# A quantizer's levels redistributed over three engines, with a transposed router product and a reordered hand-over between two phases

## The chip, the cores and the metric

The kernel runs on one core of a Trainium2 chip. The metric is the device time of one execution in microseconds (us). The engines are named as the profile names them: PE is TensorE (matrix products), DVE is VectorE, ACT is ScalarE, POOL is GpSimd, and SP is SyncE, whose queue only issues transfers here. Each engine executes its own instructions in the order in which the program wrote them; engines wait for each other through semaphores.

## The reference

All values are fp32. A weight matrix of 2048 x 2048 is quantized to a codebook of 32 values, and the result is multiplied on to two further matrices before it meets the 4096 tokens:

```python
lora_delta = lora_B @ lora_A * 0.5
cb = codebook / max(|codebook|)
normalized = (weight + lora_delta) grouped by 128 / exp(scale_log)
idx = searchsorted((cb[:-1] + cb[1:]) / 2, normalized)      # 31 thresholds
w = (cb[idx] - normalized) + normalized
w_eff = w * scale + lora_delta
y = x @ w_eff.T
...
result = y @ W_base.T + b_base
ax, probs = y @ A_w.T, softmax(y @ router_w.T)               # 16 and 8 columns
mixed = sum over experts of probs[e] * (ax @ cores[e])
out = x + result + mixed @ B_w.T * 2
```

## The kernel before

The kernel folds the matrices together first. **Phase one** forms the combined weight W_base times w_eff (plus the identity, which brings the "x +"), and the 24 router columns (16 of A_w, 8 of router_w) times w_eff. **Phase two** multiplies the tokens by the combined weight, in a two-level Strassen-like scheme of 49 block products for each of 4 token groups (line 902), which read their weights as pieces `s` from a scratch tensor `s_dram` in DRAM.

Phase one walks over 16 strips of w_eff, i = 0 to 15, each 128 x 2048. A strip lies in two tiles: `w`, the normalized weights, and `a`, the quantized result. The quantizer raises `a` from the lowest codebook value through the 31 sorted thresholds: a level r adds the r-th rise wherever w lies above the r-th threshold. For most levels this is a pair (`raise_to`, lines 527 to 535): ACT makes a mask from `w` by a Relu against the threshold, in bf16, and DVE copies the next value into `a` under the mask. Two mask buffers exist, so ACT can be at most about one mask ahead of DVE. One such pair is called a **step** here; the first copy of a strip is step 0.

The lowest levels of strip i+1 are done during strip i by other means. Before the change these are levels 0, 1 and 2: ACT does level 0 in three operations on each half of the strip (`level_0`, lines 505 to 514: Relu, Sign, then scale and bias into `a`), POOL does levels 1 and 2 on each half with a compare-and-multiply into `lv` and an add into `a` (`more_levels`, lines 516 to 522). So strips 1 to 15 have 28 steps, r = 3 to 30. Strip 0 starts at r = 2.

The order of all other work is written out by hand: `behind(n, f, ...)` (line 719) puts a call into the program after step n of strip i, and so into the queue of every engine that the call uses. During strip i, the following run beside the copies:

- For strip i+1: its load (`load_w`), the low-rank part on PE (`delta`), its scaling on ACT (`scaled`, line 496) and normalizing on POOL (`normalize`, lines 498 to 501), then the lowest levels.
- For strip i-1: after the last copy POOL finishes a strip by `straight_through` (lines 544 to 554, three operations on each half). PE then multiplies its `a` with four column blocks of W_base, first the pair (2, 0), then the pair (3, 1), each in four chunks c = 0 to 3 (`products`, line 703, with `multiply` at line 594 and `low_rank` with its products at line 589). The last chunk of (3, 1) runs at the start of strip i+1. Between the pairs comes `multiply_router` (lines 609 to 616).
- Each of these five results lies in one of only three rotating PSUM buffers. ACT empties them: `keep` (line 618) copies one column block out and SP stores it to the scratch tensor `wc_dram`; `keep_router` (line 623) copies the router's columns to `rac`. In strip i the blocks 3 and 1 of strip i-2 are kept at steps 5 and 6, the blocks 2 and 0 of strip i-1 at steps 17 and 19, the router at 22.
- `load_route` and `route` (lines 627 to 645): four transfers of 512 KB of x, and 8 products of the router columns with them, for a whole strip at once.
- From strip 5 on POOL forms Strassen sums of finished columns (`outer_w`, `inner_pair`), which are fetched (`fetch`, line 303) and stored to `s_dram` (`put`, line 340).

**The passage** stands between the phases. The last strips' columns must go through `wc_dram`, be fetched (`late_columns`, line 677; `last_fetch` for the blocks 1 and 3, line 1127), summed on DVE and put to `s_dram` through POOL's queue, while SP also issues the loads of x (xA, xB, xC) and of `s` for the first products of line 902. Three `s` buffers exist; product n uses piece s_n, and `load_s(n + 3)` stands behind product n in the program. Lines 1127 to 1141 give the order: s_0 to s_2, then `last_fetch(1)`, `last_fetch(3)`, then the load of xB.

Of the kernel before, what the change touches and what calls it, by code (L numbers as in the profile page):

```python
# [20 lines left out]
P = 128  # L21
BIG = 3.0e38
LORA_SCALE = 32.0 / 64.0
MIX_SCALE = 32.0 / 16.0


def quantizer_tables(nc, work, const, psum, cb, index, beside):
# [107 lines left out]
    base = const.tile([P, 5], F32, name="base")  # L135
    v.tensor_tensor(base[:, 0:1], step[:, 0:1], cb[:, 0:1], ALU.subtract)
    next(beside, None)
    v.tensor_copy(base[:, 2:3], step[:, 0:1])
    next(beside, None)
    v.tensor_tensor(base[:, 1:2], step[:, 1:2], base[:, 2:3], ALU.subtract)  # L140
    next(beside, None)
    v.tensor_copy(base[:, 3:4], step[:, 1:2])
    next(beside, None)
    v.tensor_tensor(base[:, 3:4], step[:, 2:3], base[:, 3:4], ALU.subtract)
    next(beside, None)
    v.tensor_scalar(base[:, 2:5:2], neg_t[:, 1:3], -1.0, None, ALU.mult)
    next(beside, None)
    return neg_t, step, base
# [34 lines left out]
def adaln_ffn_kernel(  # L183
# [72 lines left out]
    nc.gpsimd.memset(rac, 0.0)  # L256
    cb = const.tile([P, K], F32, name="cb")
    ident = const.tile([P, P], F32, name="ident")
    ones = const.tile([P, 1], F32, name="ones")

# [7 lines left out]
    def constants():  # L268
        make_identity(nc, ident)
        nc.gpsimd.memset(cores_sb, 0.0)  # L270

        nc.gpsimd.tensor_copy(ones, ident[:, Q : Q + 1])
        for j in range(1, 4):
            nc.gpsimd.tensor_tensor(ones, ones, ident[:, RP * j + Q : RP * j + Q + 1], ALU.add)
        for j in range(4):
            nc.sync.dma_start(cores_sb[:, j, 0:Q], cores)
            for rows, what in ((slice(RP * j, RP * j + Q), bwT), (slice(RP * j + Q, RP * j + Q + 1), bias)):
                nc.sync.dma_start(
                    bw_sb[rows].rearrange("q (f n) p -> q f n p", n=2),
                    what.rearrange("q (f j n p) -> q j f n p", j=4, n=2, p=P)[:, j],  # L280
                )
# [21 lines left out]
    def fetch(g, b):  # L303
        for j in range(4):
            ih, col = j // 2, j % 2
            nc.sync.dma_start(
                cols[g, b]["up"][:, ih::2, col],
                wc_dram[g][b][:, j].rearrange("p (h a) c -> p h a c", a=2),
            )
# [52 lines left out]
    with ExitStack() as sa:  # L362
# [4 lines left out]
        xsp = sa.enter_context(tc.tile_pool(name="xsp", bufs=4))  # L367
# [61 lines left out]
        with tc.tile_pool(name="tables", bufs=1) as tables:  # L429
# [20 lines left out]
            neg_t, step, base = quantizer_tables(nc, tables, const, psum_t, cb, index, first_scales)  # L450
# [23 lines left out]
        ra_sb = cl.tile([P, NM, NRA], F32, name="ra_sb")  # L474
        nc.sync.dma_start(ra_sb, raT)
# [29 lines left out]
        def level_0(i, f, part):  # L505
            q, a = half(i, f, "w"), half(i, f, "a")
            if part == 0:
                strips[i]["sg"] = mpool0.tile([P, NM // 2, P], BF16, tag="sg", name=f"sg_{i}_{f}")
                nc.scalar.activation(strips[i]["sg"], q, AF.Relu, bias=neg_t[:, 0:1])  # L509
# [3 lines left out]
            if part == 2:  # L513
                nc.scalar.activation(a, sg, AF.Identity, bias=cb[:, 0:1], scale=base[:, 0:1])  # L514

        def more_levels(i, f):
            a = half(i, f, "a")
            lv = mpool0.tile([P, NM // 2, P], F32, tag="lv", name=f"lv_{i}_{f}")
            v = nc.gpsimd
            for c in (1, 3):  # L520
                v.tensor_scalar(lv, half(i, f, "w"), base[:, c + 1 : c + 2], base[:, c : c + 1], ALU.is_gt, ALU.mult)  # L521
                v.tensor_tensor(a, a, lv, ALU.add)  # L522
# [14 lines left out]
        def quantize(i, at):  # L537

            for r in range(3 if i else 2, T):
                raise_to(i, r, new_mask(i, r), 0, 1)  # L540
                for do in at.get(r - 3, []):
                    do()

# [14 lines left out]
        lora_r = cl.tile([R, NRA], F32, name="lora_r")  # L558
# [19 lines left out]
        def lora_router():  # L578
            ps = psum_m.tile([P, OQ], F32, tag="m", name="lc_r")
            for m in range(NM):  # L580
                nc.tensor.matmul(
                    ps[:R, :NRA], lora_B_sb[:, m, :], ra_sb[:, m, :], start=(m == 0), stop=(m == NM - 1)
                )
            nc.scalar.mul(lora_r, ps[:R, :NRA], LORA_SCALE)
# [24 lines left out]
        def multiply_router(i):  # L609
            ps = psum_m.tile([P, OQ], F32, tag="m", name=f"m_{i}_r")  # L610
            for m in range(NM):
                nc.tensor.matmul(
                    ps[:, :NRA], strips[i]["a"][:, m, :], ra_sb[:, m, :], start=(m == 0), stop=False
                )
            nc.tensor.matmul(ps[:, :NRA], strips[i]["la"][:R], lora_r, start=False, stop=True)
            strips[i]["r"] = ps

# [5 lines left out]
        def keep_router(i):  # L623
            nc.scalar.copy(rac[:, strip[i], 0:NRA], strips[i]["r"][:, :NRA])


        def load_route(i):
            strips[i]["x"] = []
            for n in range(4):
                x = xsp.tile([P, 2 * HT], F32, tag="xs", name=f"xs_{i}_{n}")  # L630
                nc.sync.dma_start(x, xT[ts(strip[i], P), ts(n, 2 * HT)])
                strips[i]["x"].append(x)

        def route(i):
            for n in range(8):
                j = n % 4
                nc.tensor.matmul(
                    acc[n // 4][RP * j : RP * j + RP],
                    rac[:, strip[i], :],
                    strips[i]["x"][n // 2][:, ts(n % 2, HT)],  # L640
# [36 lines left out]
        def late_columns():  # L677

            t = big0.tile([P, NM, OQ], F32, tag="wb", name="late").rearrange("p m o -> p (m o)")
            for n, b in enumerate((0, 2)):  # L680
                f = t[:, 3584 * n : 3584 * n + 3584]
                columns(NK - 1, b, f[:, 0:2048], f[:, 2048:3584])
                fetch(NK - 1, b)
            for b in (0, 2):
# [12 lines left out]
                last_put(b, (5, 6), (2, 7), (3,), (4,))  # L697

# [17 lines left out]
        for i in range(NS):  # L716
# [5 lines left out]
            if i > 1:  # L722

                products(i - 2, (3, 1), NC - 1)
                route(i - 2)
                behind(5, keep, i - 2, 3)
                behind(6, keep, i - 2, 1)
            if i + 1 < NS:
# [5 lines left out]
                for f, (a, b, c) in enumerate(((10, 12, 14), (16, 18, 20))):  # L734
                    behind(a, level_0, i + 1, f, 0)
                    behind(b, level_0, i + 1, f, 1)
                    behind(c, level_0, i + 1, f, 2)
                    behind(c, more_levels, i + 1, f)
                behind(11, scaled, i + 1, 1)
                behind(11, normalize, i + 1, 1)  # L740
            if i > 0:


                behind(9, load_route, i - 1)
                for c in range(2):
                    behind(2 + 3 * c, products, i - 1, (2, 0), c)
                if i + 1 < NS:
                    behind(7, delta, i + 1, 1)
                for c in range(2, NC):
                    behind(2 + 3 * c, products, i - 1, (2, 0), c)  # L750
                behind(13, multiply_router, i - 1)
                behind(17, keep, i - 1, 2)
                behind(19, keep, i - 1, 0)
                for c in range(NC - 1):
                    behind((17, 20, 22)[c], products, i - 1, (3, 1), c)
                behind(22, keep_router, i - 1)
                if i + 2 < NS:
                    behind(20, load_la, i + 2)
            else:
# [3 lines left out]
                behind(24, lora_columns, 1)  # L763
                behind(26, lora_router)
            for n, (g, b) in enumerate(made.get(i, [])):
                step_of = (4, 9, 11, 12, 15, 26, 27) if len(made[i]) == 1 else (
# [31 lines left out]
        route(last - 1)  # L798
        keep(last - 1, 3)
        keep(last - 1, 1)  # L800
        load_route(last)
# [4 lines left out]
        for bs in ((2, 0), (3, 1)):  # L806
            for c in range(NC):
                products(last, bs, c)
            if bs[0] == 2:
                multiply_router(last)  # L810
            for b in bs:
                keep(last, b)
            if bs[0] == 2:
                keep_router(last)
                late_columns()
        route(last)
# [286 lines left out]
    at(early, 1, lambda g: load_x("xC", g, 1, 1))  # L1103
# [23 lines left out]
    def last_fetch(b, t):  # L1127
        buf = home[t].tile([P, 4096], F32, tag=t, name=f"last_{b}")
        columns(NK - 1, b, buf[:, 0:2048], buf[:, 2048:3584])
        fetch(NK - 1, b)  # L1130
# [8 lines left out]
    last_fetch(1, "C12")  # L1139
    last_fetch(3, "U2")  # L1140
    load_x("xB", 0, 0, 1)
# [18 lines left out]
    for n in range(total + 1):  # L1160
# [12 lines left out]
        if n + 3 < total and n < total:  # L1173
            load_s(n + 3)
        if 1 <= n <= total:
# [52 lines left out]
```

## Time and profile before

Three runs took 2699.41, 2703.0 and 2703.13 us; the median is 2703.0. The profiled execution took 2701.32 us, with a span of 2699.5 and a mean granted TensorE clock of 0.971.

| engine | busy us | share of the span | instructions |
|---|---|---|---|
| PE matmul | 2562.5 | 95% | 10544 |
| PE weight load | 1761.5 | 65% | 10544 |
| DVE | 1574.9 | 58% | 995 |
| ACT | 1117.8 | 41% | 740 |
| POOL | 1300.1 | 48% | 751 |

| operation, shape | engine | count | mean ns |
|---|---|---|---|
| masked copy, 128x2048 (line 533) | DVE | 449 | 2479 |
| mask, 128x2048 (line 532) | ACT | 449 | 1998 |
| Relu, Sign, scale and bias, 128x1024 (509, 512, 514) | ACT | 30 each | 1133, 1043, 1231 |
| compare and multiply, 128x1024 (521) | POOL | 60 | 3782 |
| add, 128x1024 (522) | POOL | 60 | 2375 |
| column block out of PSUM, 128x512 (620) | ACT | 64 | 568 |

A duration in such a table is the time from an operation's start to its end. Operations of one engine can overlap a little, so where they run back to back the distance from start to start counts, and it is shorter: a mask takes 1998 ns, but the next operation starts 1.90 us after it. The page's shares are averages over two phases with different limits: DVE is busy nine tenths and more of each slice until about 1190 us, and two to four tenths afterwards. Ends of matmuls are modelled, so PE's 95% does not say that PE is the limit.

### The profile page before, as it was taken

To read this page: it belongs to the slowest core of one execution; us is meant where nothing else is said; L and a number is where in the kernel's file an instruction comes from. 1 tells how busy PE (TensorE), PEld (TensorE's weight loads), DVE (VectorE), ACT (ScalarE), POOL (GpSimd) and SP (SyncE) were. 2 spreads that over 40 slices of the span, in tenths; PEclk is the share of its full clock that TensorE was granted. 3 is DMA by queue.
4 is the path that set the end of the run, shared out by engine and by line. 5 is a ranking of instruction groups with operands and counts; after the bars stand their busy time and mean duration, and the time that the engine had idled before them with its cause. 6 is when DMAs were issued, how large, how long until landed. Compare 5 with 4: busy or idle time off the path is not lost.

```text
span 2699.5 us, 26233 instructions
## 1 busy us (share of the span) xinstructions
PE 2562.5 (95%) x10544; PEld 1761.5 (65%) x10544; DVE 1574.9 (58%) x995; ACT 1117.8 (41%) x740; POOL 1300.1 (48%) x751
## 2 busy tenths in 40 slices
PE   4699999999999999999799999999999999999999
PEld 2244444444444444445688888888888888888887
DVE  9999999999999999973423213233123322224321
ACT  6888988999998888840000000000000000000000
POOL 5666668889888888744304232033310313302324
PEclk9799999999999999999899999999999999999999
DMA  7345457766776767699744666545675455854554
GB/s 283 138 167 178 178 174 246 233 229 225 244 242 232 244 219 237 209 314 324 300 174 143 231 245 217 208 142 209 213 264 186 171 206 181 292 194 171 186 198 163
DMA packets 222809, 581.06 MB, mean 215 GB/s; under 512 B 18328, under 2 KB 120608, under 8 KB 177760
## 3 DMA queue, kind: packets, MB, share of 16 engines
q1 hardware_dynamic: 216448, 559.01, 60.2%
q0 software_dynamic: 4640, 13.90, 1.4%
q10 hardware_dynamic: 1600, 6.49, 0.6%
q8 instruction: 83, 1.36, 0.2%
q14 instruction: 38, 0.31, 0.0%
HBM read 477.62 MB, written 101.71 MB: 215 GB/s over the span
## 4 chain that ended last, share of the span: by engine, by line
PE 59%; DVE 22%; ACT 8%; DMA 5%; issue 3%; SPq 2%; POOL 1%; DVEq 0%; POOLq 0%; ACTq 0%
PE z L902 49%; DVE a L533 21%; PE m L601 8%; ACT above L532 6%; PE z L932 1%; DMA wbp<-in_wbT 1%; DMA s<-s_dram 1%; DMA xA<-in_xT 1%; ACT out L620 1%; DMA s_dram<-late_z 1%; ACT a L514 1%; SPq L347 1%; SPq L348 0%; DMA s_dram<-z 0%; ACT sg L509 0%
## 5 line engine op out<-in xcount | busy, mean ns | idle before, releaser
L533 DVE COPY_PREDICATED a<-above,step 128x2048 f32<-128x2048 uint16 (+1 forms) x453 | 1116.5, 2468 | 51.1 <-ACT above L532 5.7
L532 ACT ACTIVATE above<-w,neg_t 128x2048 bf16<-128x2048 f32 (+1 forms) x453 | 899.4, 1991 | 141.7 <-DVE a L533 128.8
L902 PE MATMUL z<-t,s 128*128 128x256 f32 x3584 | 793.5, 381 | 7.1 <-DMA s<-s_dram 7.1
L902 PEld LDWEIGHTS z<-t,s 128*128 128x128 f32 x3584 | 679.1, 190 | 110.9 <-issue 20.0
L601 PE MATMUL m<-wbp,a 128*128 128x512 f32 x1024 | 506.7, 641 | 43.0 <-POOL a L554 35.7
L601 PE MATMUL m<-wb,a 128*128 128x512 f32 x1024 | 467.0, 599 | 26.6 <-ACT out L620 26.6
L601 PEld LDWEIGHTS m<-wbp,a 128*128 128x128 f32 x1024 | 205.7, 206 | 294.4 <-issue 243.9
L601 PEld LDWEIGHTS m<-wb,a 128*128 128x128 f32 x1024 | 194.7, 192 | 276.6 <-issue 238.7
L982 ACT COPY m<-z 128x1024 f32<-128x1024 f32 x28 | 28.4, 1013 | 766.0 <-PE z L902 766.0
L902 PE MATMUL z<-xA,s 128*128 128x256 f32 x1152 | 256.2, 381 | 12.4 <-DMA s<-s_dram 12.4
L993 POOL TENSOR_TENSOR c<-u,m 128x1024 f32<-128x1024 f32 x16 | 50.1, 3129 | 444.1 <-DVE u L990 422.8
L902 PEld LDWEIGHTS z<-xA,s 128*128 128x128 f32 x1152 | 219.8, 191 | 43.7 <-issue 13.6
L521 POOL TENSOR_SCALAR lv<-w,base 128x1024 f32<-128x1024 f32 x60 | 226.9, 3782 | 3.7
L993 POOL TENSOR_TENSOR M<-u,m 128x1024 f32<-128x1024 f32 x8 | 25.7, 3208 | 354.1 <-DVE u L990 296.4
L902 PE MATMUL z<-xB,s 128*128 128x256 f32 x768 | 169.7, 379 | 0.0
L902 PE MATMUL z<-xC,s 128*128 128x256 f32 x768 | 169.7, 379 | 0.0
L984 DVE TENSOR_TENSOR u<-z,m 128x1024 f32<-128x1024 f32 x28 | 34.3, 1223 | 219.0 <-issue 175.5
L902 PEld LDWEIGHTS z<-xB,s 128*128 128x128 f32 x768 | 145.9, 190 | 19.8
L902 PEld LDWEIGHTS z<-xC,s 128*128 128x128 f32 x768 | 145.9, 190 | 19.8
L988 ACT COPY m<-z 128x1024 f32<-128x1024 f32 x28 | 28.3, 1011 | 308.5 <-PE z L902 308.5
L522 POOL TENSOR_TENSOR a<-a,lv 128x1024 f32<-128x1024 f32 x60 | 142.5, 2375 | 18.4 <-ACT a L514 13.8
L552 POOL TENSOR_TENSOR a<-a,w 128x1024 f32<-128x1024 f32 x30 | 71.3, 2376 | 144.3 <-DVE a L533 144.3
(206 smaller groups left out, 1916.6 us busy)
## 6 DMA issues: line engine op xcount, KB each, us to landing
s<-s_dram SPq DMA_DIRECT2D x196, 1024.0 KB, 4.9
wbp<-in_wbT SPq DMA_DIRECT2D x131, 1024.0 KB, 5.2
xs<-in_xT SPq DMA_DIRECT2D x64, 512.0 KB, 7.2
xA<-in_xT SPq DMA_DIRECT2D x24, 1024.0 KB, 9.9
s_dram<-z SPq DMA_DIRECT2D x84, 256.0 KB, 5.6
xB<-in_xT SPq DMA_DIRECT2D x16, 1024.0 KB, 10.6
outT<-M SPq DMA_DIRECT2D x16, 1024.0 KB, 12.7
w<-in_weight SPq DMA_DIRECT2D x15, 1024.0 KB, 7.3
```

The costliest lines, as they stand in the source:

```text
L347: q.dma_start(to[:, n, 1:3, g, c], y[:, n, 1])
L521: v.tensor_scalar(lv, half(i, f, "w"), base[:, c + 1 : c + 2], base[:, c : c + 1], ALU.is_gt, ALU.mult)
L522: v.tensor_tensor(a, a, lv, ALU.add)
L532: nc.scalar.activation(above[:, c], q, AF.Relu, bias=neg_t[:, r : r + 1])
L533: nc.vector.copy_predicated(a, above[:, c].bitcast(U16), step[:, r : r + 1].to_broadcast([P, F // n]))
L552: v.tensor_tensor(a, a, w, ALU.subtract)
L601: nc.tensor.matmul(ps, strips[i]["a"][:, CM * c + m, :], t[:, m, :], start=c == 0 and m == 0, stop=False)
L902: nc.tensor.matmul(z[:, c, :], s[:, k, ts(c, P)], rhs[:, k, :], start=not more and k == 0 and c % PER == 0, stop=k == NK - 1 and c % PER = ...
L982: nc.scalar.copy(temp("m1", o), z["a"])
L984: nc.vector.tensor_tensor(temp("u2", o), z["b"], state["m1", o], ALU.add)
L988: nc.scalar.copy(temp("m5", o), z["c"])
L993: lambda d: nc.gpsimd.tensor_tensor(d, state["u3", o], state["m5", o], ALU.add),
```

## The change

- **Levels.** `quantizer_tables` now returns tables for five levels (`rise`, `past`; NL = 5). `first_step(i)` replaces the fixed 3: strips 1 to 5 begin at level 5 and have 26 steps, strips 6 to 15 begin at level 4 and have 27. Level 0 stays with ACT on both halves. Levels 1 up to the last but one are POOL's (`pool_levels`: three levels in strips 1 to 5, two in strips 6 to 15). The last of these extra levels is done by ACT on the first half (`scalar_level`, three operations into `lx`) and by DVE on the second half (`vector_level`, one compare-and-multiply into `lx`); POOL adds `lx` to `a` (`last_level`). The steps at which they stand change too (`LV`).
- **Router.** The product is transposed: the router's columns, padded from 24 to 32, are the stationary operand and the strip moves. The 16 partial products go to four groups of 32 PSUM partitions. ACT copies the 128 x 128 result to `raw` (`router_parts`, step 16), and one product with a matrix of stacked identities (`stack`) adds the four groups and turns the result back (`router_sum`, step 17), before `keep_router` at 22.
- **Route.** It is done in two halves of four products, the second at step 8 of the next strip, with two x buffers instead of four. In the last strip the second half of x goes to the mask buffers.
- **Keeps.** The blocks 2 and 0 are kept at steps 14 and 15 instead of 17 and 19; the chunks of the pair (3, 1) stand at 16, 19 and 21 instead of 17, 20 and 22. Some of POOL's sums and their stores move by one or two steps.
- **Passage.** `late_columns` fetches the last quarter of both blocks behind the other three quarters. `last_fetch(3)` is issued from POOL's queue. The load of xB moves behind product 0 and s_3, that of xC from the first group's product 1 to product 4.

```diff
+        def first_step(i):
+            return 2 if i == 0 else 5 if i < 6 else 4
+
+        def scalar_level(i, f, r, part):
             q, a = half(i, f, "w"), half(i, f, "a")
...
+            if part == 2 and r == 0:
+                nc.scalar.activation(a, sg, AF.Identity, bias=cb[:, 0:1], scale=rise[:, 0:1])
+            elif part == 2:
+                strips[i]["lx"] = mpool0.tile([P, NM // 2, P], F32, tag="lx", name=f"lx_{i}_{f}")
+                nc.scalar.activation(strips[i]["lx"], sg, AF.Copy, scale=rise[:, r : r + 1])
+
+        def level(v, lv, i, f, r):
+            v.tensor_scalar(lv, half(i, f, "w"), past[:, r : r + 1], rise[:, r : r + 1], ALU.is_gt, ALU.mult)
+
+        def pool_levels(i, f):
             a = half(i, f, "a")
             lv = mpool0.tile([P, NM // 2, P], F32, tag="lv", name=f"lv_{i}_{f}")
-            v = nc.gpsimd
-            for c in (1, 3):
-                v.tensor_scalar(lv, half(i, f, "w"), base[:, c + 1 : c + 2], base[:, c : c + 1], ALU.is_gt, ALU.mult)
-                v.tensor_tensor(a, a, lv, ALU.add)
+            for r in range(1, first_step(i) - 1):
+                level(nc.gpsimd, lv, i, f, r)
+                nc.gpsimd.tensor_tensor(a, a, lv, ALU.add)
+
+        def vector_level(i, f):
+            strips[i]["lx"] = mpool0.tile([P, NM // 2, P], F32, tag="lx", name=f"lx_{i}_{f}")
+            level(nc.vector, strips[i]["lx"], i, f, first_step(i) - 1)
+
+        def last_level(i, f):
+            a = half(i, f, "a")
+            nc.gpsimd.tensor_tensor(a, a, strips[i]["lx"], ALU.add)
...
-            for r in range(3 if i else 2, T):
+            for r in range(first_step(i), T):
...
             for m in range(NM):
+                j = m % 4
                 nc.tensor.matmul(
-                    ps[:, :NRA], strips[i]["a"][:, m, :], ra_sb[:, m, :], start=(m == 0), stop=False
+                    ps[RP * j : RP * j + RP, 0:P], ra_sb[:, m, :], strips[i]["a"][:, m, :],
+                    start=m < 4, stop=m >= NM - 4 and j > 0, tile_position=(0, RP * j),
+                    skip_group_check=True,
                 )
...
+        def router_parts(i):
+            nc.scalar.copy(raw, strips[i]["r"][:, 0:P])
+
+        def router_sum(i):
+            nc.tensor.matmul(strips[i]["r"][:, P : P + RP], raw, stack, start=True, stop=True)
...
+        LV = ((9, 11, 12), (13, 15, 16), (17, 19, 21))
...
-                route(i - 2)
+                route(i - 2, 0)
+                behind(0, load_route, i - 2, 1)
...
-                for f, (a, b, c) in enumerate(((10, 12, 14), (16, 18, 20))):
-                    behind(a, level_0, i + 1, f, 0)
-                    behind(b, level_0, i + 1, f, 1)
-                    behind(c, level_0, i + 1, f, 2)
-                    behind(c, more_levels, i + 1, f)
-                behind(11, scaled, i + 1, 1)
+                for r, f, parts in ((0, 0, LV[0]), (first_step(i + 1) - 1, 0, LV[1]), (0, 1, LV[2])):
+                    for n, p in enumerate(parts):
+                        behind(p, scalar_level, i + 1, f, r, n)
+                behind(10, scaled, i + 1, 1)
                 behind(11, normalize, i + 1, 1)
+                behind(13, pool_levels, i + 1, 0)
+                behind(19, last_level, i + 1, 0)
+                behind(20, pool_levels, i + 1, 1)
+                behind(22, vector_level, i + 1, 1)
+                behind(23, last_level, i + 1, 1)
...
+                if i > 1:
+                    behind(8, route, i - 2, 1)
...
-                behind(17, keep, i - 1, 2)
-                behind(19, keep, i - 1, 0)
+                behind(14, keep, i - 1, 2)
+                behind(15, keep, i - 1, 0)
                 for c in range(NC - 1):
-                    behind((17, 20, 22)[c], products, i - 1, (3, 1), c)
+                    behind((16, 19, 21)[c], products, i - 1, (3, 1), c)
+                behind(17, router_sum, i - 1)
                 behind(22, keep_router, i - 1)
+                behind(16, router_parts, i - 1)
...
-    at(early, 1, lambda g: load_x("xC", g, 1, 1))
+    at(early, 4, lambda g: load_x("xC", g, 1, 1))
...
-    last_fetch(1, "C12")
-    last_fetch(3, "U2")
-    load_x("xB", 0, 0, 1)
+    last_fetch(1, "C12", nc.sync)
+    last_fetch(3, "U2", nc.gpsimd)
...
+        if n == 0:
+            load_x("xB", 0, 0, 1)
```

`ra_sb` is now cleared by a memset on DVE before its load, since 8 of its 32 columns are not loaded.

## The prediction

> **What bounds the kernel now.** The profiled execution took 2701.3 us, of which 2699.5 are the span; the sums below are made against it, and the median of the runs shown, 2703.0, lies 1.7 higher. I read the page's chain of waits first: TensorE (PE) 59%, VectorE (DVE) 22%. By time it is two kernels. From about 1308 us on PE runs line 902 nearly without a gap, and the change touches none of that work. Up to 1188 us the strips are quantized. So I read one strip on each engine, timelines in order of time (start us, us, engine, line, idle before).
>
> ```profile
> 715.11 40.98 DVE L533 COPY_PREDICATED a<-above,step 128x2048 f32<-128x2048 uint16 x16 [0.27 <-ACT above L532]
> ...
> 681.43 2.38 POOL L552 TENSOR_TENSOR a<-a,w 128x1024 f32<-128x1024 f32 x1 [9.23 <-DVE a L533]
> ...
> 753.80 2.38 POOL L552 TENSOR_TENSOR a<-a,w 128x1024 f32<-128x1024 f32 x1 [8.88 <-DVE a L533]
> ```
>
> DVE does masked copies back to back: (40.98-2.48)/15 = 2.57 us each. From straight_through to straight_through a strip takes 72.4, which is 28 x 2.57 = 72.0 plus 0.4 of waits. GpSimd (POOL) is done 9 us before the strip ends. So a strip is DVE's 28 copies. ScalarE (ACT) makes a mask in 1.90 (two take 3.88 with the tail) and may be one mask ahead (two buffers); its gaps before masks sum to 118.6 us over the 15 strips, 7.9 per strip.
>
> Then what PE delivers to ACT (strip start S = 681.24, the first copy):
>
> ```profile
> 694.09 3.70 PE L601 MATMUL m<-wb,a 128*128 128x512 f32 x8 [1.30 <-ACT out L620]
> ...
> 719.61 1.13 PE L589 MATMUL m<-lora_c,la 64*128 64x512 f32 x4
> 720.67 3.75 PE L612 MATMUL m_r<-ra_sb,a 128*128 128x24 f32 x32
> 724.35 0.40 PE L615 MATMUL m_r<-lora_r,la 64*128 64x24 f32 x2
> 725.67 6.68 PE L601 MATMUL m<-wbp,a 128*128 128x512 f32 x8 [0.92 <-ACT out L620]
> ...
> 725.06 0.56 ACT L620 COPY out<-m 128x512 f32<-128x512 f32 x1
> ```
>
> Column block 0 cannot start before the keep at step 5 has freed its PSUM buffer (694.09), and the pair (2, 0) is then solid PE work until 720.7. The keep of block 2, at step 17, comes at 725.06, some 4 us after its product.
>
> **Levels moved.** Per strip the change takes away two copies (strips 1 to 5) or one (6 to 15): 5.1 or 2.6 us of DVE. It adds one DVE tensor_scalar over 128x1024 in strips 0 to 14, which the trace does not show. The nearest row, a DVE TENSOR_TENSOR of that size, takes 1.22. The Trainium skill, VectorE: DVE Perf Modes, perf-mode tier table, says that an fp32 tensor_scalar in SBUF runs at 2x and a two-input op does not (1227 ns for 2048 elements); half of that with its fixed part is an estimate of 0.7. The row has two inputs, so I take 0.7, with 1.22 as the other end. It counts in 11 strips only (below), so 6 us by the choice. DVE's own account, 15 x 2.57 + 5 x 2.57 = 51 saved and 10 paid, would give 41 us, if nobody else were late.
>
> ACT gains three operations per strip (relu 1.04, sign 0.95, scale 1.13 between starts: 3.1) for one or two masks of 1.90. POOL, for strips 1 to 5, gets per half 3 levels and a last add for 2 levels: 12.3 to 21.
>
> **The keeps at steps 14 and 15.** This decides. ACT is in order, and masks stand behind the keep. PE: straight_through's first half is ready at S+7.0. In the new kernel PE has by then idled 7 us or more, because it ends the old strip near S-1; after such idling it starts at half clock (strip 1: the first 8 matmuls take 6.45 from start to start instead of 3.5, after 26.6 us idle; at 1307.62 the same after 7.1). So block 0 starts at S+7.0+6.4 = S+13.4 (S+12.8 if warm). Then 25.52 (694.09 to 719.61), 0.93 for the half of the route moved in there (1.85/2), and 1.16 from L589's start to the ACT copy (1255.50 to 1256.66): the keep of 2 can start at **S+41.0**. ACT gets there at S+37.0: mask 14 starts at 13 x 2.57 = 33.4, plus 1.7 that ACT is late after steps 9 to 13, each with an operation of about 1 us against a slack of 0.67, plus 1.9. It waits 4.0 us. Mask 15 then starts at 41.55, and copy 15 2.02 later at 43.6 instead of 38.55: DVE is 5.0 behind. Steps 15 to 17 cost ACT 3.37, 3.18 and 2.93 (mask plus sign and keep, scale and router copy, relu) against 2.57, another 1.8. Lag 6.8.
>
> - Strips 6 to 14: 27 x 2.57 + 0.7 + 6.8 = 76.9, against 72.4: **+4.5 each, 40.5**.
> - Strip 5: 26 x 2.57 + 0.7 + 6.8 = 74.3: +1.9. Strip 15 (no next levels): 27 x 2.57 + 5.0 = 74.4: +2.0.
> - Strips 1 to 4: the second half's first level is done by ACT at step 21: mask at 58.2, +1.9+1.23 = S+61.4. POOL then has add, level, add, level, add, last add:
>
> ```profile
> 154.02 2.38 POOL L522 TENSOR_TENSOR a<-a,lv 128x1024 f32<-128x1024 f32 x1 [2.77 <-ACT a L514]
> 156.50 3.78 POOL L521 TENSOR_SCALAR lv<-w,base 128x1024 f32<-128x1024 f32 x1
> 160.37 2.37 POOL L522 TENSOR_TENSOR a<-a,lv 128x1024 f32<-128x1024 f32 x1
> 174.14 2.38 POOL L552 TENSOR_TENSOR a<-a,w 128x1024 f32<-128x1024 f32 x1 [11.40 <-DVE a L533]
> ```
>
>  that is 4 x 2.46 + 2 x 3.87 = 17.5, so the next strip's first copy waits until S+78.9, though DVE is ready at 74.3: **+6.5 each, 26**. For 4-level strips POOL needs 11.2 after S+61.4 and is in time.
> - Strip 0: 0.7 and 1.6 of crowded ACT steps, +2.3; the DVE memset of ra_sb +0.5 (POOL's memset of that size takes 0.53).
>
> Phase one: +73 us.
>
> **Router.** Before, 32 matmuls at 117 ns (3.75). After, 32 with 32-column weights at four positions: route's rows (1.92 for 16 of 512 columns) give the same 117, a quarter of 128 columns about 60; 1.9 to 3.75, and one more product. The 6.68 for 8 matmuls behind it (3.5 warm) is PE at half clock; wider moving data may keep it at full clock, 3.1 a strip. None of it is on the path here: PE ends before the next strip's data. The extra ACT copy is counted above; the sum matrix is built in POOL's idle time after 27 us.
>
> **Passage.** After strip 15, PE begins 2.3 behind DVE's end (before 4.9), gets no half clock behind the router (-1.9), waits about 1 for the router copy and keep, has half a route more (0.9) and starts half-clocked (+3): about -0.4. Then
>
> ```profile
> 1265.42 13.98 PE L902 MATMUL z<-t,s 128*128 128x256 f32 x64
> 1291.82 8.67 PE L902 MATMUL z<-xA,s 128*128 128x256 f32 x32 [12.42 <-DMA s<-s_dram]
> 1307.62 9.29 PE L902 MATMUL z<-t,s 128*128 128x256 f32 x32 [7.13 <-DMA s<-s_dram]
> ...
> 1266.03 0.36 SPq L306 DMA_DIRECT2D last<-wc_dram  x1
> 1273.60 2.93 SPq L306 DMA_DIRECT2D last<-wc_dram  x4
> 1276.64 1.13 SPq L850 DMA_DIRECT2D xB<-in_xT  x2
> 1277.86 1.24 SPq L856 DMA_DIRECT2D s<-s_dram  x1
> ```
>
> SP stands until 1273.6 for the second fetch's buffer; xB, s3, xC and s4 wait behind it. From 1279.4 to 1316.75 two products take 37.4 instead of 13.8: 23.5 to be had. After, s3 may go out at 1266.4, ahead of xB, 13 us before its use, and s4 at 1272.5, 14 before. The Trainium skill, DMA: Bandwidth & Descriptors, "Issuing engines are not separate DMA queues", speaks against it: moving an issue to another queue saves the sequencer's time only. If landings stayed as they are (s3 14.0, s4 26.8 us), 1 and 13 us of stall would remain and 9 be gained; but s4's 26.8 had xB, s3 and xC before it, and now has xC behind it. I take 20, ends 9 and 23.5. The fetch on POOL's queue stands behind the late puts, as it did on SP; last_put behind it starts 4 us later, but its data are first used by product 7, at about 1311, after landing near 1296.
>
> Sum: 2701.3 + 73 - 20 - 0.4 = **2754**.
>
> **Rivals.** (A) Faster: the keep's wait is not there, because the product of 2 is done by S+37. PE would have to be 4.0 us earlier, and that is the point from which it decides. For it: PE's busy share says little. Against it: from 694.09 PE has no gap. With the crowded steps and POOL's lateness left in, phase one is +11, the total 2692; without these too, 2660. (B) Nothing gained in the passage beyond 9, and the vector level at 1.22: 2754 + 11 + 6 = 2771, at most 2785. (C) PE warm (S+12.8, -8), the lag half of 6.8 (-45), all 23.5 gained: about 2698, no change.
>
> **Chances.** Forecast 0.65 (its own range 2730 to 2770), A 0.20, B 0.10, C 0.05. Range 2690 to 2785: it leaves out most of A. A measurement tells 0.2%, 5.4 us, from no change. Faster 0.21, same 0.03, slower 0.76.
>
> **What would show it.** Right: strips of 77 us from 6 on, 79 in 1 to 4; ACT idle at L620 for PE L589, about 4 a strip; DVE idle for ACT at step 15; in strips 1 to 4 DVE idle for POOL; no waits for s at the start of line 902's products. Wrong: strips under 72 us, or a keep of 2 that starts without a wait.

## The result, and the profile after

The changed kernel took 2885.6 us (median of four runs, 2884.3 to 2887.0), the kernel before 2702.9 (now four runs, 2699.4 to 2703.1). The ratio is 1.068, with a 95% interval of 1.066 to 1.070. The forecast was 2754, with a range up to 2785. The direction was right; the loss is three and a half times as large as forecast.

The profiled execution took 2884.31 us, with a span of 2882.5, 183.0 above the span before. Phase one takes some 188 us more and the stretch behind it 5.5 less, read from the timelines:

| stretch | before, us | after, us | difference | forecast |
|---|---|---|---|---|
| start of the span to strip 0's straight_through | 101.2 | 119.5 | +18.4 | +2.8 |
| strips 1 to 4, each (straight_through to straight_through) | 72.5 | 87.7 | +15.2 | +6.5 |
| strip 5 | 72.4 | 80.3 | +7.9 | +1.9 |
| strips 6 to 14, each | 72.5 | 83.7 | +11.2 | +4.5 |
| strip 15, to the end of the last copy | 72.2 | 73.1 | +0.9 | +2.0 |
| last copy's end to the end of the span | 1511.2 | 1505.7 | -5.5 | -20.4 |

The chain of waits of the changed kernel, by engine, as shares of the span:

```profile
PE 55%; POOL 24%; ACT 6%; DVE 6%; DMA 4%; issue 4%; SPq 0%; DVEq 0%; POOLq 0%
```

Before, DVE had 22% of this chain and POOL 1%. Now POOL has 24%, though POOL has gaps in every strip. So the chain runs through POOL's work because somebody waits for it. Who that is shows first in the list of waits (us in total, times, longest), two rows of the changed kernel and one of the kernel before:

```profile
ACT a L519 <- POOL a L532: 150.5, 15, 16.2
DVE a L551 <- ACT above L550: 254.0, 146, 16.3
...
DVE a L533 <- ACT above L532: 5.7, 20, 0.7
```

One strip shows how the two are linked. ACT's timeline in strip 7 of the changed kernel, whose first copy starts at S = 634.72 (start us, us, engine, line, operation; in brackets the idle time before and what ended it):

```profile
660.30 1.15 ACT L514 ACTIVATE sg<-w,neg_t 128x1024 bf16<-128x1024 f32 x1 [2.97 <-POOL w L424]
...
675.66 0.59 ACT L653 COPY out<-m 128x512 f32<-128x512 f32 x1 [0.72 <-PE m L608]
...
702.43 1.24 ACT L519 ACTIVATE a<-sg,cb,rise 128x1024 f32<-128x1024 bf16 x1 [7.80 <-POOL a L532]
703.58 1.99 ACT L550 ACTIVATE above<-w,neg_t 128x2048 bf16<-128x2048 f32 x1
```

DVE's timeline in the same strip:

```profile
663.38 2.49 DVE L551 COPY_PREDICATED a<-above,step 128x2048 f32<-128x2048 uint16 x1 [2.89 <-ACT above L550]
...
687.52 10.23 DVE L551 COPY_PREDICATED a<-above,step 128x2048 f32<-128x2048 uint16 x4 [0.43 <-ACT above L550]
705.60 2.48 DVE L551 COPY_PREDICATED a<-above,step 128x2048 f32<-128x2048 uint16 x1 [7.85 <-ACT above L550]
707.98 0.80 DVE L525 TENSOR_SCALAR lx<-w,past,rise 128x1024 f32<-128x1024 f32 x1
```

And POOL's:

```profile
693.72 2.37 POOL L532 TENSOR_TENSOR a<-a,lv 128x1024 f32<-128x1024 f32 x1
696.19 3.78 POOL L525 TENSOR_SCALAR lv<-w,past,rise 128x1024 f32<-128x1024 f32 x1
700.05 2.34 POOL L532 TENSOR_TENSOR a<-a,lv 128x1024 f32<-128x1024 f32 x1
708.92 2.37 POOL L540 TENSOR_TENSOR a<-a,lx 128x1024 f32<-128x1024 f32 x1 [6.52 <-DVE lx L525]
```

Read them together. POOL's last add of its own levels ends at 702.39, and ACT's write of level 0 into the same half starts at 702.43, after 7.80 idle. The mask for step 22 stands behind that write in ACT's queue and ends at 705.57; DVE's copy starts at 705.60, after 7.85 idle. DVE's own level, behind that copy, then makes POOL wait 6.52. Over phase one ACT waits 150.5 us for line 532, once in each of the strips 0 to 14, and longest, 14.0 to 16.2, in the strips 0 to 4, where POOL does three levels. DVE's waits for masks sum to 254.0 us; before they were 5.7.

The program text gives the reason. `pool_levels(i + 1, 1)` stands behind step 20, ACT's third operation of level 0 behind step 21 (`LV`, last number). Both write the second half of `a`. What is later in the program waits for what is earlier: ACT for POOL. In the kernel before, both stood behind the same step with ACT's write first, and it was POOL that waited (2.77 us at 154.02, in a row that the prediction shows). (ACT's write also replaces what POOL had added to that half, so that in the changed kernel this half lacks POOL's levels.)

The passage on PE's timeline:

```profile
1443.06 1.92 PE L672 MATMUL acc<-xs,rac 128*32 128x512 f32 x16
1462.91 8.98 PE L957 MATMUL z<-xA,s 128*128 128x256 f32 x32 [17.93 <-DMA s<-s_dram]
1471.73 13.98 PE L957 MATMUL z<-t,s 128*128 128x256 f32 x64
```

And on SP's queue, which issues the loads:

```profile
1445.05 1.06 SPq L905 DMA_DIRECT2D xA<-in_xT  x2
1446.21 4.14 SPq L911 DMA_DIRECT2D s<-s_dram  x3
```

Behind the rows shown the products follow each other without a gap (1485.54, 1492.45, 1499.35): the waits for s of 12.42 and 7.13 us that stood there before are gone, as forecast. But the very first product now waits 17.93. xA is issued at 1445.05, just when the last product of route is done; before, it was issued at 1207.3, 51 us ahead of its use. By the program's layout of its buffers, which no trace prints, xA lies in part on one of the mask buffers, and the changed kernel puts the last quarter of the last strip's x into that buffer. e5_x below tests this.

### The profile page after: what moved, and what is told of

The parts are those of the page before. It is cut to its first block, busy times and chain, and to the rows that moved or that the text cites. A ratio compares the mean times of both kernels' runs of the same rounds, so it can differ in the third digit from the quotient of the medians.

```text
span 2882.5 us, 26431 instructions
## 1 busy us (share of the span) xinstructions
PE 2512.0 (87%) x10576; PEld 1711.4 (59%) x10576; DVE 1534.4 (53%) x989; ACT 1125.7 (39%) x781; POOL 1430.9 (50%) x808
## 3 DMA queue, kind: packets, MB, share of 16 engines
q10 hardware_dynamic: 1600, 6.49, 0.6%
## 4 chain that ended last, share of the span: by engine, by line
PE 55%; POOL 24%; ACT 6%; DVE 6%; DMA 4%; issue 4%; SPq 0%; DVEq 0%; POOLq 0%
PE z L957 47%; POOL lv L525 9%; PE m L620 6%; POOL a L532 6%; DVE a L551 6%; ACT above L550 4%; DMA w<-in_weight 4%; POOL w L501 1%; POOL a L572 1%; POOL a L571 1%; POOL a L540 1%; PE z L987 1%; POOL w L424 1%; ACT a L519 1%; POOL a L573 1%
## 5 line engine op out<-in xcount | busy, mean ns | idle before, releaser
L551 DVE COPY_PREDICATED a<-above,step 128x2048 f32<-128x2048 uint16 (+1 forms) x433 | 1066.4, 2467 | 280.2 <-ACT above L550 254.0
L550 ACT ACTIVATE above<-w,neg_t 128x2048 bf16<-128x2048 f32 (+1 forms) x433 | 859.7, 1991 | 119.1 <-DVE a L551 106.4
L620 PE MATMUL m<-wb,a 128*128 128x512 f32 x1024 | 461.2, 593 | 1.9 <-ACT out L653 1.8
L957 PE MATMUL z<-xA,s 128*128 128x256 f32 x1152 | 256.4, 381 | 17.9 <-DMA s<-s_dram 17.9
L525 POOL TENSOR_SCALAR lv<-w,past,rise 128x1024 f32<-128x1024 f32 x70 | 264.5, 3779 | 4.2
L532 POOL TENSOR_TENSOR a<-a,lv 128x1024 f32<-128x1024 f32 x70 | 165.5, 2364 | 5.8
L957 PEld LDWEIGHTS z<-xC,s 128*128 128x128 f32 x768 | 146.2, 190 | 19.6
## 6 DMA issues: line engine op xcount, KB each, us to landing
xB<-in_xT SPq DMA_DIRECT2D x16, 1024.0 KB, 10.2
```

The costliest lines, as they stand in the source:

```text
L525: v.tensor_scalar(lv, half(i, f, "w"), past[:, r : r + 1], rise[:, r : r + 1], ALU.is_gt, ALU.mult)
L532: nc.gpsimd.tensor_tensor(a, a, lv, ALU.add)
L550: nc.scalar.activation(above[:, c], q, AF.Relu, bias=neg_t[:, r : r + 1])
L551: nc.vector.copy_predicated(a, above[:, c].bitcast(U16), step[:, r : r + 1].to_broadcast([P, F // n]))
L620: nc.tensor.matmul(ps, strips[i]["a"][:, CM * c + m, :], t[:, m, :], start=c == 0 and m == 0, stop=False)
L957: nc.tensor.matmul(z[:, c, :], s[:, k, ts(c, P)], rhs[:, k, :], start=not more and k == 0 and c % PER == 0, stop=k == NK - 1 and c % PER = ...
```

## The experiments

**e1_order: which way the wait points.** One number of the changed kernel is changed.

```diff
-        LV = ((9, 11, 12), (13, 15, 16), (17, 19, 21))
+        LV = ((9, 11, 12), (13, 15, 16), (17, 19, 20))
```

> The changed kernel with one number changed: ACT's third operation of level 0 on the second half (the write of a, line 519) stands at step 20 instead of 21, and so in the program ahead of POOL's levels on the same half, which stand at step 20 too. Now POOL waits for ACT, as I had assumed in the prediction, and not ACT for POOL. Theory (in the changed kernel the write at 21 waits for POOL's adds at 20, and masks and copies queue behind it): ACT's wait at line 519 for line 532, 150 us over the 15 strips, is gone; strips 6 to 14 take about 77 us instead of 84, strips 1 to 4 about 76 to 79 instead of 87.7; total 2750 to 2785. Rival (the steps on ACT are too many, wherever they stand; or the keeps at 14 and 15 cost it): the wait only changes its name, strips stay above 82 us, total above 2860. This kernel's second half holds POOL's levels; in the changed kernel ACT's later write puts level 0 alone in their place.

Measured: 2762.3 us (2758.2 to 2764.9), ratio to before 1.023 (1.021 to 1.025). Strips 1 to 4 take 76.8, strips 6 to 14 also 76.8, the first stretch 103.5. Two rows of ACT's timeline in strip 8 of this kernel:

```profile
665.18 1.15 ACT L514 ACTIVATE sg<-w,neg_t 128x1024 bf16<-128x1024 f32 x1 [3.58 <-POOL w L424]
...
696.59 1.24 ACT L519 ACTIVATE a<-sg,cb,rise 128x1024 f32<-128x1024 bf16 x1
```

The write has no idle time before it any more, and 123 us are gone with one step's shift. The theory holds, the rival falls. What is left is a strip of 76.8 against 72.5. One part of it is neither ACT nor the keeps: DVE's own level, 0.80 us in the changed kernel, now falls beside POOL's adds and takes 2.5 to 2.9 in the strips 7, 10, 12 and 14.

```profile
626.17 2.90 DVE L525 TENSOR_SCALAR lx<-w,past,rise 128x1024 f32<-128x1024 f32 x1
```

These four strips take 77.8 in the mean, the other five from 6 to 14 take 76.1.

**e2_keeps and e7_router_late: the keeps.** e2_keeps is e1_order with the keeps back in their old places:

```diff
-                behind(14, keep, i - 1, 2)
-                behind(15, keep, i - 1, 0)
+                behind(17, keep, i - 1, 2)
+                behind(19, keep, i - 1, 0)
...
-                    behind((16, 19, 21)[c], products, i - 1, (3, 1), c)
-                behind(17, router_sum, i - 1)
+                    behind((17, 20, 22)[c], products, i - 1, (3, 1), c)
+                behind(20, router_sum, i - 1)
...
-                behind(16, router_parts, i - 1)
+                behind(18, router_parts, i - 1)
```

> The kernel of e1_order with the keeps of the blocks 2 and 0 back at the steps 17 and 19, the chunks of (3, 1) back at 17, 20 and 22, and router_parts and router_sum at 18 and 20. Theory (the prediction's own: the keep at 14 makes ACT wait about 4 us for PE): 4 us a strip less than e1_order in strips 5 to 14, some 40 to 55 us in all, and 2700 to 2735. Rival (the trace of the changed kernel has only 1 us of wait at the keep, because ACT is already 2 to 3 us late from step 9, where its Relu waits for POOL's normalizing): 1 to 2 us a strip at most, and 2735 to 2770.

Measured: 2766.5 us (2754.8 to 2768.9); nothing is gained. The experiment had a fault of its own, which ACT's timeline shows:

```profile
701.21 0.19 ACT L657 COPY rac<-m_r 128x32 f32<-128x32 f32 x1 [5.17 <-PE m_r L649]
```

The router's sum, moved to step 20, lies on PE behind a chunk of (3, 1), and the copy at step 22 waits for it, 64.6 us over the 15 strips. So e7_router_late moves that copy away:

```diff
-                behind(22, keep_router, i - 1)
+                behind(25, keep_router, i - 1)
```

> The kernel of e2_keeps with keep_router at step 25 instead of 22. In e2_keeps ACT waited 3.1 to 5.3 us a strip there for router_sum, which I had put on PE behind a chunk of (3, 1); that wait is the new one that may have hidden what moving the keeps back is worth. Theory (the keeps at 14 and 15 cost about 4 us a strip and e2_keeps only traded one wait for another): strips 5 to 14 fall from 77.2 to 73 to 74, total 2725 to 2740. Rival (ACT is late by its own work, so that a wait taken from it comes back in the following steps in part): strips 75 to 76.5, total 2745 to 2760.

Measured: 2744.2 us (2741.2 to 2748.1), strips 6 to 14 at 75.6. That lies between the two theories, nearer to the rival. Against e1_order the keeps' places, with the chunks of (3, 1) and the router's steps that moved along, are worth 18 us, 1.2 a strip, and not 4. Even that is not the keeps' alone: DVE's 15 levels take 24.3 us in all in e1_order and 17.0 here, because they fall elsewhere beside POOL's adds. No run separates the two.

**e8_relu: the Relu at step 9.** In the strips of e7_router_late one wait of ACT is left that is not for DVE:

```profile
ACT sg L514 <- POOL w L424: 30.4, 15, 4.8
```

(us in total, times, longest.) e8_relu moves the first half's operations, level 0 and the extra level, behind POOL's normalizing:

```diff
-        LV = ((9, 11, 12), (13, 15, 16), (17, 19, 20))
+        LV = ((11, 12, 13), (14, 15, 16), (17, 19, 20))
```

> The kernel of e7_router_late with ACT's operations of the first half at the steps 11, 12 and 13 (level 0) and 14, 15 and 16 (extra level) instead of 9, 11, 12 and 13, 15, 16. At step 9 the Relu waited 2 to 3 us a strip for POOL's normalizing, which ends later than that; no other wait is left on ACT there. Theory (that wait is the rest of ACT's lateness): strips 6 to 14 fall from 75.4 by 2 to 73.5, total 2720 to 2730. Rival (ACT's slack of 0.67 us a step is used up: six operations of about 1.05 us now stand in six steps running, and the wait comes back as lateness): strips 74.5 to 75.5, total 2736 to 2746.

Measured: 2725.2 us (2723.0 to 2729.2), strips 6 to 14 at 73.6. The theory holds. DVE's waits in phase one, from the list of waits:

```profile
DVE a L551 <- ACT above L550: 60.9, 125, 1.1
DVE a L551 <- POOL a L540: 13.9, 4, 3.5
```

In the changed kernel the first of these rows stands at 254.0, with 16.3 as the longest. Now it is many small delays of up to 1.1: no single wait, but ACT's operations themselves, as e9_all below bears out. The second row is the strips 1 to 4, whose POOL chain of three levels ends after the copies.

**e3_vector: ACT's operations.** On e1_order, the extra level of the first half goes from ACT to DVE:

```diff
-                for r, f, parts in ((0, 0, LV[0]), (first_step(i + 1) - 1, 0, LV[1]), (0, 1, LV[2])):
+                for r, f, parts in ((0, 0, LV[0]), (0, 1, LV[2])):
...
+                behind(16, vector_level, i + 1, 0)
```

> The kernel of e1_order with the extra level on DVE in both halves (a second compare-and-multiply at step 16); ACT's three operations for it, 3.3 us a strip at the steps 13, 15 and 16, are gone. Theory (what keeps a strip of e1_order at 76.8 instead of 70.1 to 72 is ACT: between the steps 9 and 19 each step costs ACT a mask and one more operation, 3.0 us against DVE's 2.57, and it starts late by the wait at step 9): ACT's lag falls by 2 to 3 us a strip and DVE gets 0.7 more, strips 6 to 14 take 74 to 75.5; POOL bounds strips 1 to 4 as before; total 2735 to 2750. Rival (the wait for POOL's normalizing and the keep of block 2 set the pace, ACT's operation count does not): strips 77 to 78, total 2762 to 2775.

Measured: 2745.4 us (2743.1 to 2746.1), strips 6 to 14 at 75.5. Giving DVE, the engine that sets the pace, more work made the kernel 17 us faster, because it took 3.3 us a strip from ACT, which was late: DVE's waits for masks fall from 102.3 us in e1_order to 74.6.

**e4_passage and e5_x: the passage.** e4_passage is the kernel before with the change's passage alone, but for the order in `late_columns`, which stays as it was:

```diff
-    at(early, 1, lambda g: load_x("xC", g, 1, 1))
+    at(early, 4, lambda g: load_x("xC", g, 1, 1))
...
-    last_fetch(3, "U2")
-    load_x("xB", 0, 0, 1)
+    last_fetch(3, "U2", nc.gpsimd)
...
+        if n == 0:
+            load_x("xB", 0, 0, 1)
```

> The kernel before with the passage's edits alone: the second of the two last fetches issued from POOL's queue, xB loaded behind product 0 and s_3, xC behind product 4. Theory (these edits are worth what the prediction took, and the changed kernel lost most of it because its load of x for phase two comes late): 20 us less, 2675 to 2690. Rival (landings are bound by the transfers themselves, not by their place in the queue): 0 to 9 us less, 2693 to 2703.

Measured: 2682.5 us (2681.5 to 2686.0), ratio 0.993 (0.992 to 0.995): 19.6 less. PE's timeline:

```profile
1258.86 7.17 PE L902 MATMUL z<-xA,s 128*128 128x256 f32 x32
...
1303.58 7.17 PE L902 MATMUL z<-t,s 128*128 128x256 f32 x32 [3.01 <-DVE u L984]
```

No product waits for s; the next thing late is a sum on DVE, 3.01. So the edit is worth what the forecast took, where nothing else is in its way. e5_x is the changed kernel with the last quarter of x elsewhere:

```diff
+                if i == NS - 1 and h == 1 and n == 1:
+                    x = mpool0.tile([P, NM // 2, P], F32, tag="lx", name=f"xs_{i}_{h}{n}").rearrange("p m i -> p (m i)")
-                if i == NS - 1 and h == 1:
+                elif i == NS - 1 and h == 1:
                     x = mpool.tile([P, F], BF16, tag="above", name=f"xs_{i}_{h}{n}").bitcast(F32)
```

> The changed kernel with one buffer moved: the last quarter of the last strip's x goes to the free buffer lx instead of the mask buffer. That mask buffer lies at bytes 159968 to 164064 of a partition, inside the place of xA for phase two (147104 to 163488), so that in the changed kernel xA, and s_0 to s_2 behind it on SP, are issued only when the last product of route has read the mask buffer, at 1445. Theory: xA goes out some 60 us earlier, s_0 to s_2 some 15 us earlier, the 17.9 us wait at the first product of line 957 shrinks to 0 to 5, and the time falls by 10 to 18 us, to 2867 to 2876. Rival (the pieces s_0 to s_2 or the later s pieces wait for POOL's stores in any case): within 5 us of the changed kernel, 2880 to 2887.

Measured: 2875.4 us (2873.2 to 2876.0), 10.2 below the changed kernel. PE's timeline of e5_x:

```profile
1446.77 7.17 PE L959 MATMUL z<-xA,s 128*128 128x256 f32 x32
...
1494.95 9.22 PE L959 MATMUL z<-t,s 128*128 128x256 f32 x32 [5.70 <-DVE u L1041]
```

The first product waits for nothing. On SP's queue xA goes out at 1425.59, some 20 us earlier and not 60, because SP issues `late` ahead of it until 1425.5; that was enough. Of the 17.9 us only 10.2 are gained, since a wait for DVE's sum, 5.70, stands further on. From the last copy's end to the end of the span e5_x takes 1494.7 us, e4_passage 1491.3, before 1511.2.

**e6_router: the router alone.** The kernel before with the transposed product, and route in halves with three x buffers:

```diff
-        xsp = sa.enter_context(tc.tile_pool(name="xsp", bufs=4))
+        xsp = sa.enter_context(tc.tile_pool(name="xsp", bufs=3))
...
+                behind(18, router_parts, i - 1)
+                behind(19, router_sum, i - 1)
                 behind(22, keep_router, i - 1)
```

> The kernel before with the router's edits alone: its product transposed, the partial sums added by one more product (copies at step 18, sum at 19), and route in two halves, with three x buffers. Theory (PE is not what a strip waits for): the product's 32 matmuls take 1.1 us instead of 3.75, the half clock behind them stays (6.7 us for the next 8), ACT has 0.3 us more, strips stay at 72.2 to 73, and the total is within 5 us of before, 2697 to 2708. Rival (ACT's copy waits for PE at step 18, or the sum is late for step 22): each strip 1 to 3 us longer, 2715 to 2745.

Measured: 2704.8 us (20 runs, 2701.7 to 2707.8), ratio 1.0012 (1.0005 to 1.0019), which is within 0.2% of no change. Strips stay at 72.5; the stretch behind the last copy is 4.2 longer (1515.4 against 1511.2). PE's timeline:

```profile
722.17 1.08 PE L619 MATMUL m_r<-a,ra_sb 128*32 128x128 f32 x32
...
726.18 5.40 PE L606 MATMUL m<-wbp,a 128*128 128x512 f32 x8 [2.59 <-ACT out L639]
```

The product shrinks from 3.75 to 1.08 us, and PE then waits 2.59 for a keep instead. The 8 products behind it take 5.40, at a granted clock of 0.66 to 0.71, not the 6.7 that I expected (before, 6.68 at 0.50 to 0.60).

**e9_all and c1_level: what the levels can bring.** e9_all puts the repairs together: e8_relu, with the edits of e3_vector and e5_x (the buffer is `lv` here).

> The kernel of e8_relu with the extra level on DVE in both halves, as in e3_vector, and the last quarter of the last strip's x in the free buffer lv, as in e5_x: all four repairs together. Theory (they add up: 17 us by DVE's second level as between e1_order and e3_vector, 10 by the buffer as between the changed kernel and e5_x, from what e8_relu takes): 2693 to 2717; strips 1 to 4 stay at 75 to 77, because POOL's 17.5 us of three levels behind ACT's write at step 20 end after the copies, so that the five-level strips keep it at or above the kernel before less the passage's 20. Rival (ACT is no longer late in any case once one of the repairs is in, so that they overlap): 2718 to 2735.

Measured: 2709.4 us (20 runs, 2701.0 to 2714.1), ratio 1.0028 (1.0021 to 1.0035). The time lies in the theory's range, but the last two repairs add 16 us to e8_relu's gain and not the 27 that they brought apart. The repaired change is still not faster than before. With three of ACT's operations gone, DVE's waits for masks are down to 28.9 us. In its profiled execution, one of the quickest at 2703.45, strips 6 to 14 take 73.0 and strips 1 to 4 74.9. Its span is 21.8 above that of e4_passage: 9.7 of this stand in the strips 1 to 4, 3.9 in 6 to 14, 10.3 behind the last copy and 2.3 ahead of strip 0's straight_through, while the strips 5 and 15 are 4.3 shorter.

c1_level starts from e4_passage with route in two halves and three x buffers, keeps ACT's steps and the keeps of before, and takes one level from the copies in strips 1 to 15. Its edit of the levels:

```diff
+        def vector_level(i, f):
+            lx = mpool0.tile([P, NM // 2, P], F32, tag="lx", name=f"lx_{i}_{f}")
+            strips[i]["lx"] = lx
+            nc.vector.tensor_scalar(lx, half(i, f, "w"), base[:, 6:7], base[:, 5:6], ALU.is_gt, ALU.mult)
...
-            for r in range(3 if i else 2, T):
+            for r in range(4 if i else 2, T):
...
+                for f, (c, d) in enumerate(((15, 16), (21, 22))):
+                    behind(c, vector_level, i + 1, f)
+                    behind(d, last_level, i + 1, f)
```

> The kernel of e4_passage with route in two halves and three x buffers, and one level more taken from the masked copies in the strips 1 to 15: DVE does it by compare-and-multiply on both halves (0.8 us each, behind the steps 15 and 21) and POOL adds it (2.4 each); ACT's steps and the keeps stay where they were before. Theory (DVE bounds a strip as long as ACT has no more to do than before): a strip is 27 x 2.57 + 2 x 0.72 + 0.4 = 71.2 instead of 72.4, 16 us in all, 2660 to 2672. Rival (POOL, with 9 us of slack of which the adds take 4.9, or the shorter time between ACT's steps, makes the strip late): 72 to 74, 2680 to 2705.

Measured: 2669.8 us (2667.3 to 2671.3), ratio 0.988 (0.987 to 0.990): faster than both kernels, 12.7 below e4_passage. A strip takes 71.4 in the mean; the stretch behind the last copy is 7.0 longer than in e4_passage. DVE's timeline is again one long run:

```profile
641.47 0.79 DVE L529 TENSOR_SCALAR lx<-w,base 128x1024 f32<-128x1024 f32 x1
642.18 15.37 DVE L544 COPY_PREDICATED a<-above,step 128x2048 f32<-128x2048 uint16 x6
...
658.18 41.08 DVE L544 COPY_PREDICATED a<-above,step 128x2048 f32<-128x2048 uint16 x16
```

## Why the prediction was wrong

**The step that failed** is the one for the second half's first level: "POOL then has add, level, add, level, add, last add ..., so the next strip's first copy waits until S+78.9", with POOL waiting for ACT's step 21. I read the edge as if level 0 must come first because it is level 0. The program put POOL's levels one step earlier, so the edge ran the other way, and the waiting engine was ACT, behind which every mask queues. Where I charged 6.5 us in each of four strips, and nothing in the others because POOL "is in time" there, the wait is 7.7 us in the mean of the strips 5 to 14 and 14.0 to 16.2 in the strips 0 to 4. e1_order shows it: with the edge as I had assumed it, strips 1 to 4 take 76.8 (forecast 78.9), strips 6 to 14 76.8 (76.9), and the total is 2762 (2754). That the numbers then agree so well is in part luck, as the next paragraphs show.

**The keeps** were named as what decides, and that is wrong, though the number for those strips came out. In strip 7 of the changed kernel the product of block 2 was ready at S+40.9 (forecast 41.0) and copy 15 began at S+43.5 (43.6): the walk through PE was right. But ACT came at S+40.2, not at S+37.0, and waited 0.72, not 4.0; in e1_order its waits at the keeps sum to 6.7 us over all strips. It was late from the Relu at step 9: POOL's normalizing ends at S+25.5, and I had given those steps 1.7 us of lateness without looking up when their input is ready. (POOL itself had waited 2.41 there for the load of w, which SP issued at S+14.0 behind a load that waited for PE.) More than one cause thus gave the sum that I gave to one, and that the number came out is luck. By the runs the keeps' places are worth 18 us at most (e1_order to e7_router_late), the Relu's step 19 (e7_router_late to e8_relu).

**The DVE level** takes 0.80 from start to end in the changed kernel, and 0.70 from its start to the next copy's (707.98 to 708.68). So the choice of 0.7, from the Trainium skill (VectorE: DVE Perf Modes, perf-mode tier table) against 1.22 from the nearest row, was right, as long as POOL leaves DVE alone; beside POOL's adds it takes up to 2.90 (e1_order, and below).

**The router** was rightly put off the path; its product was at 1.08 outside the 1.9 to 3.75. The full clock behind it came where PE did not wait (8 products in 3.70, at a granted clock of 1.00), and PE did start the strip at half clock (6.49 after 17.88 idle, at 0.50 to 0.59).

**The passage** was rightly sized as an edit (20 against 19.6 in e4_passage) and wrong in this kernel. The forecast read the x buffers' change in words, "in the last strip the second half of x goes to the mask buffers", and did not ask what those bytes hold next. That is 10.2 us by e5_x. In the repaired kernel, e9_all, the span behind the last copy is still 10.3 us longer than in e4_passage (1501.6 against 1491.3). What makes that up was not tried and stays open. Two differences are in question: route in halves (e6_router and c1_level, which have it, are 4.2 and 7.0 longer there than the kernels that they start from), and the new order in `late_columns`, which e4_passage lacks.

**The rivals** all lay at or below 2785; none of them had this wait. Rival A's condition, ACT not kept by PE, was even met in part, and the strip was long all the same. (Its second figure, 2660, seems to leave out the passage: 2701 less 41 of DVE's account and less 20 is about 2640.)

## What to carry to other kernels

When two engines write the same tile, look up which instruction stands first in the program before saying who waits; the sense of the computation does not tell it, and one step decided 123 us here. A wait on the engine that feeds the bound costs the bound all that the feeder cannot catch up: here ACT gains 0.67 us a step (2.57 less 1.90), so it can carry one operation of 1 us in every step and a half, and not one in each. When a buffer is reused for something new, list what comes to lie on the same bytes afterwards, and what will wait for it.

## What the runs showed of the hardware

DVE's compare-and-multiply of 128x1024 takes 0.78 to 0.82 us in all 30 instances of c1_level, but 0.79 to 2.50 in e9_all. The longest one on DVE's timeline of e9_all:

```profile
534.80 2.50 DVE L525 TENSOR_SCALAR lx<-w,past,rise 128x1024 f32<-128x1024 f32 x1
```

POOL's timeline of e9_all at that moment:

```profile
534.39 2.36 POOL L532 TENSOR_TENSOR a<-a,lv 128x1024 f32<-128x1024 f32 x1
536.86 4.09 POOL L525 TENSOR_SCALAR lv<-w,past,rise 128x1024 f32<-128x1024 f32 x1
```

DVE's operation ends 0.55 us after POOL's add, so it seems to have stood until the add was done. The row of e1_order above is alike: POOL's add began at 626.17 too and took 2.35, and DVE's ended 0.55 after it. The Trainium skill (SBUF — State Buffer, "SBUF: two separate sides") tells of a port pair that the two share and that the first one holds for its whole instruction. These rows agree, and so do ten of the later instances of c1_level, where DVE's began up to 0.12 us ahead of a compare-and-multiply of POOL and that one took 4.29 to 4.36 instead of 3.78. But the ten instances in the strips 0 to 4 of c1_level began 1.5 to 1.8 us after the start of a compare-and-multiply of POOL, and there DVE's took 0.79 to 0.81 and POOL's 3.78 as ever, which that rule would not give. In the changed kernel none of DVE's 15 overlapped with POOL, since POOL was waiting for it.
